# Where a unit's key rows are fetched in a streamed two-layer cross attention

## The chip, the cores and the metric

The kernel runs on one core of a Trainium2 chip. A core has a matrix engine (TensorE, PE in the profile, with weight loads shown as PEld), VectorE (DVE), ScalarE (ACT), GpSimd (POOL) and SyncE (SP). Each runs its own list of instructions in order; semaphores hold an instruction until what it needs is done. Nearly all DMA copies of this kernel are issued by SyncE, one after the other. An issue takes some 0.4 to 0.6 us of SyncE; the copy itself runs on 16 DMA engines. An issue that waits for a semaphore holds up every later issue of SyncE.

The metric is the device time of one execution in microseconds. Before the change it is 3652.42 us, the median of 3 runs (3637.54 to 3652.66).

## The reference

A Perceiver-like stack of two layers works on 32 batches of 64 query tokens of width 256, and attends in each layer to a context of 1601 tokens per batch. Cut to what matters here:

```
x = x + L0_xattn(layernorm(x), ctx, ctx, ...)   # 16 heads of 16, 1601 keys
x = x + L0_attn(layernorm(x), ...)              # self attention over 64 tokens
x = x + L0_ffn(layernorm(x), ...)               # top-k routed attention
x = x + L1_xattn(layernorm(x), ctx, mask, ...)  # cross attention again, masked
x = x + L1_attn(layernorm(x), ...)              # quantised self attention
x = x + L1_ffn(layernorm(x), ...)               # product-key experts
```

In a cross attention, q, k and v are projections of x and of the context, scores are q.k for each head, a softmax runs over the 1601 keys (in layer 1 the masked ones are left out), and the result is the weighted sum of v. Each batch of the context is gone through once per layer, 64 batch passes in all. Almost the whole time goes into these two cross attentions; the small stages of layer 0 are woven in between.

## The kernel before, in words

`stream` (from line 509) does both cross attentions as one stream. The work is cut in **units**: unit `u` is four heads of one batch pass, `b, q4 = divmod(u, 4)`, so there are `NU` = 256 units, some 12 us each. Keys reach a unit in three hops:

- **Projection.** `projections` (L1069) walks 416 pairs of 128-token context blocks, each with index `i`. `load(i)` (L970, issue at L974) brings `raw` into one of three buffers. `split(i)` (L982) makes `chi` on ScalarE (L986) and `clo` on GpSimd (L987). `keys(i)` runs 24 matmuls into `kp` (L1089) and adds the bias on VectorE (L1095); `values(i)` does the same for v (L1117, L1122).
- **Parting.** `parted(i)` (L1032) cuts a key block into three bf16 parts `ks` (ScalarE L1039 and L1046, GpSimd L1040 and L1041) and stores them to a DRAM scratch `kd` (L1049), a ring of four batches.
- **Fetch.** `fetch(u)` (L1187) gathers a unit's rows from `kd` into `kst`, one of three buffers (`kring[u % 3]`): four copies of 208 KB (L1203), four of 104 KB (L1208), 1248 KB together, and in layer 1 a ninth of 25.1 KB with the mask (L1213).

What `keys`, `split` and `parted` have left to do is kept in lists, and `tick()` (L1005) hands out a little of it: first the raw loads that are due, then, for each pending generator, one stage (a parting's first half, its second half, its store, or a split). `fetch(u)` first calls `tick(b)` for its own batch, which hands out a stage of the others too, and finishes all that batch `b` still owes. `keys_values` (L1300) draws further projection steps until a target that grows by a twelfth of a batch per step is met.

The order of everything is written out by hand in the loop over units (L1417). Each iteration has three steps (`i` = 0, 1, 2), and a step is, in this order: maxima of the next unit's scores (`sp`, L1236, VectorE L1241), weighted sums of the last step's probabilities (`acc`, L1292), this step's score products (`tp`, L1277, with ScalarE's exponential `e`, L1282), then `group_step`, `end_step` (small pieces of the other stages; the twelve `qst` copies of L632 that bring new queries every 16 units come from here), `tick()` and `keys_values`. The third step computes the products `p5` and `p6`, the last that read the unit's `kst` buffer, and ends with a second `group_step`.

At the top of iteration `u`, `fetch(u + 2)` is called:

```
                if u + 2 < NU and u + 2 not in ksts:
                    fetch(u + 2)
```

Its buffer is that of unit `u - 1`, whose last products stand in the third step of the iteration before. The first reader of the fetched rows is `maxima(u + 2)`, at the start of iteration `u + 1`. The copies wait on SyncE for those last products and, for a batch's first unit, for the batch's last store to `kd`.

Of the kernel before, what the change touches and what calls it, by code (L numbers as in the profile page):

```python
# [61 lines left out]
class Kernel:  # L62
# [446 lines left out]
    def stream(self):  # L509
        nc, tc, ins = self.nc, self.tc, self.ins  # L510
        with ExitStack() as ctx:
# [25 lines left out]
            def layer(b):  # L537
                return b // NB
# [5 lines left out]
            def halves(x):  # L544
                return x.rearrange("(r p) h n -> r p h n", r=2)
# [446 lines left out]
            kds, vs, ksts, cuts, loads, due = {}, {}, {}, [], [], []  # L992
# [12 lines left out]
            def tick(b=-1):  # L1005


                if b < 0:
                    due[:], rest = loads[:], due[:]
                    del loads[:]  # L1010
                    for one in rest:
                        one()
                left = 2
                for one in list(cuts):
                    work = one[1] == "work"
                    if one[0] > b and work:
                        if left == 0:
                            continue
                        left -= 1
                    while True:  # L1020
                        one[1] = next(one[2], None)
                        if one[1] is None:
                            cuts.remove(one)
                        if one[1] is None or one[0] > b:
                            break
# [161 lines left out]
            def fetch(u):  # L1187

                b, q4 = divmod(u, 4)
                while keyed.get(b, 0) < NCH:  # L1190
                    made[0] += next(proj)
                tick(b)
                k = kring[u % 3]
                if u == 2:

                    for r in (32, 96):
                        nc.sync.dma_start(k[r : r + 32 : 2], kring[0][r : r + 32 : 2])

                kh = halves(k).rearrange("r p (a j) n -> r a p (j n)", a=2)
                d = kds[b][:, 16 * q4 : 16 * q4 + 16]  # L1200
                for rows, part in ((FIRST, 0), (THIRD, 1)):
                    for r in range(2):
                        nc.sync.dma_start(  # L1203
                            halves(k)[r, rows].rearrange("p h n -> p (h n)"), d[part]
                        )
                for a in range(2):
                    for r in range(2):
                        nc.sync.dma_start(  # L1208
                            kh[r, a, SECOND],
                            d[0 if r == a else 2, :, 2 * a * NKP : 2 * a * NKP + 2 * NKP],  # L1210
                        )
                if layer(b) == 1:
                    nc.sync.dma_start(  # L1213
                        k[MASKR : P : 64, :, :NKE],
                        self.rows[b % NB, :NKE].unsqueeze(0).unsqueeze(0)
                        .to_broadcast([2, 4, NKE]),
                    )
                ksts[u] = k
# [48 lines left out]
            def probabilities(u, i):  # L1267

                q, h0, tok = tokens(u)
                k = ksts[u]  # L1270
                two = min(2, NCH - 2 * i)
                m = min(P, NK - 2 * i * P)
                sp = ps_t.tile([P, 2, 4, NQ], F32, tag="tp", name=f"tp{u}_{i}")
                for c in range(two):
                    k0 = (2 * i + c) * P
                    for h in range(4):
                        nc.tensor.matmul(  # L1277
                            sp[:m, c, h, :], k[:, 2 * (h % 2) + h // 2, k0 : k0 + m], q[:, h0 + h, tok],
                            start=True, stop=True,
                        )  # L1280
                e = pt.tile([P, 2, 4, NQ], F32, tag="e", name=f"e{u}_{i}")
                nc.scalar.activation(e[:m, :two], sp[:m, :two], AF.Exp)  # L1282
                return e

            def weighted(u, i, e):

                b, q4 = divmod(u, 4)
                slot = 2 * q4 + b % 2
                for c in range(2 * i, min(2 * i + 2, NCH)):
                    m = min(P, NK - c * P)  # L1290
                    for h in range(4):
                        nc.tensor.matmul(  # L1292
                            acc[32 * h : 32 * h + 17, slot, :], vs[b, c][:m, 4 * q4 + h, :],
                            e[:m, c - 2 * i, h, :], start=(c == 0), stop=(c == NCH - 1),
                        )

            NU = 2 * NB * 4
# [14 lines left out]
            def prepare():  # L1312

                for which, n in (("L1_attn_w_qkv", 24), ("L1_attn_w_out", 8)):
                    got = self.sc.tile([P, n], F32, tag=f"wm{n}", name=f"{which}_m")
                    yield from self.weight_max(bg, which, got)
                    yield from self.weight_grid(which, got, bank)
                    yield from self.weight_round(bg, which)
                yield from self.temperature()

            def end_step():

                for queue in (ends, spare):
                    while queue:
                        n, t, steps = queue[0]
                        if next(steps, True) is None:
                            return
                        queue.pop(0)
                        if n == 1:
                            spare.append((2, t, self.twice_normed(small, bg, t)))  # L1330
                        elif n == 0 and t % 2 == 1:
                            g = t // 2
                            groups.append((128 + 16 * g - 2, self0(g)))
                            groups.append((128 + 16 * g - 1, ffn0(g)))
# [57 lines left out]
            def banks_made(n):  # L1392
                for _ in range(n):
                    made[0] += next(proj)
                    tick()
# [16 lines left out]
            for i, _ in enumerate(maxima(0)):  # L1412
                if i < 4:
                    banks_made(1)
            groups.append((15, self.stream_setup(wp, bg, bank)))
            late = []
            for u in range(NU):  # L1417
                b, q4 = divmod(u, 4)
                if u in (2, 3, 4):
                    self.load_x(1 << (u - 1), 1 << (u - 1))  # L1420
                if u == 133:

                    assert not ends
                    nc.sync.dma_start(
                        self.bo,
                        ins[self.WNAMES[1][3] % "v"].unsqueeze(0).to_broadcast([P, D]),
                    )
                    self.bv.append(self.bo)
                if u in (8, 132):
                    spare.append((2, 0, prepare() if u == 8 else self.affine_grids(bg)))  # L1430
                if u % 16 == 1 and u + 15 < NU:
                    groups.append((u + 15, queries(*divmod((u + 15) // 16, NG))))
                if u + 2 < NU and u + 2 not in ksts:
                    fetch(u + 2)
                nat = maxima(u + 1) if u + 1 < NU else iter(())

                for i, js in enumerate(((0, 1, 2), (3, 4), (5, 6))):
                    for _ in range((2, 2, 0)[i]):
                        next(nat, None)
                    for done in late:  # L1440
                        weighted(*done)
                        if done[1] == 6 and done[0] % 8 == 7:
                            n, t = divmod(done[0] // 8, NT)
                            ends.append((n, t, finish(n, t)))
                            next(ends[-1][2])
                    if i == 2:
                        next(nat, None)
                    late = [(u, j, probabilities(u, j)) for j in js[:2]]
                    banks[0] = 0
                    group_step()  # L1450
                    end_step()
                    tick()
                    keys_values(LEAD + (3 * u + i + 1) / 12.0, 0.15)
                    late += [(u, j, probabilities(u, j)) for j in js[2:]]
                    if i == 2:
                        group_step()
                        if u % 2:
                            end_step()
                for _ in nat:
                    pass  # L1460
# [976 lines left out]
```

## Time and profile before

| what | before |
|---|---|
| median of 3 runs | 3652.42 us (3637.54 to 3652.66) |
| the profiled execution's own time | 3643.7 us |
| its span | 3642.0 us |
| mean granted TensorE clock | 0.956 |
| TensorE busy | 3316.4 us (91%) |
| VectorE busy | 2417.2 us (66%) |
| ScalarE busy | 2367.8 us (65%) |
| GpSimd busy | 1792.4 us (49%) |
| DMA moved | 651.22 MB, 179 GB/s mean |
| `kst` copies from `kd` | 1024 of 208 KB, 1024 of 104 KB |
| `raw` loads | 379 of 256 KB, 62 of 72 KB |
| stores to `kd` | 384 of 384 KB, 64 of 108 KB |

How to read it: the profile is one execution. Its chain of work that ended last runs only through the closing stages here (VectorE 7%, TensorE 2% of the span), so the stream, the first 3090 us or so, is read by the waits of its engines and by their timelines. A line of waits says which engine and line waited, for whom, then the total in us, how many times, and the longest. In a timeline a number in square brackets is the idle time of the engine before an instruction, and what ended it. SPq is SyncE's queue, where an issue's duration is not the copy's. A stretch's line gives busy time of each engine, the granted TensorE clock, the DMA engines' share and GB/s.

### The profile page before, as it was taken

The numbers are of one execution on the slowest core, as the hardware profiler recorded it, in microseconds if no ns is written. First come the engines' busy times: TensorE is split into PE (matmuls) and PEld (weight loads), VectorE is DVE, ScalarE is ACT, GpSimd is POOL, SyncE is SP. The second block draws the span as 40 slices with busy tenths as digits, with TensorE's granted clock in tenths as the row PEclk, the third lists the DMA queues.
The fourth block names the chain that finished last, engine by engine and source line by source line (L and its number), as shares of the span: only waits on it lengthen the run. The fifth ranks groups of instructions, "written<-read, shape, count | busy, mean of one in ns | idle before, by whom it ended". The sixth has DMA issues, their size and how long they took to land. (4 is left out here: it accounts for less than half of the span.)

```text
span 3642.0 us, 148306 instructions
## 1 busy us (share of the span) xinstructions
PE 3316.4 (91%) x62993; PEld 2707.7 (74%) x63007; DVE 2417.2 (66%) x6166; ACT 2367.8 (65%) x4656; POOL 1792.4 (49%) x2109
## 2 busy tenths in 40 slices
PE   6899999999999999999999999999999998775698
PEld 5678887878778787778887778878778786332467
DVE  4556665666666566566667666656666566789879
ACT  3677766767667776667676777677667676154562
POOL 2455454555545554545555655556456563003246
PEclk8999999999999999999999999999999999887699
DMA  7888777777777777777787777777778887100000
GB/s 179 214 231 230 203 191 213 205 207 201 204 193 205 211 208 214 200 198 200 204 216 210 199 209 197 195 210 202 206 206 232 231 241 194 60 1 1 1 5 20
DMA packets 616920, 651.22 MB, mean 179 GB/s; under 512 B 127216, under 2 KB 581444, under 8 KB 599684
## 3 DMA queue, kind: packets, MB, share of 16 engines
q1 hardware_dynamic: 616256, 641.73, 64.3%
q8 instruction: 495, 8.11, 1.0%
q14 instruction: 169, 1.38, 0.1%
HBM read 468.30 MB, written 171.11 MB: 176 GB/s over the span
## 5 line engine op out<-in xcount | busy, mean ns | idle before, releaser
L1241 DVE TENSOR_REDUCE mx<-sp 128x1 f32<-128x400 f32 (+1 forms) x2048 | 1031.8, 565 | 324.5 <-PE sp L1236 323.9
L1282 ACT ACTIVATE e<-tp 128x512 f32<-128x512 f32 (+1 forms) x1792 | 931.7, 565 | 465.4 <-PE tp L1277 456.4
L987 POOL TENSOR_TENSOR clo<-raw,chi 128x512 fp32r<-128x512 f32 (+1 forms) x408 | 508.3, 1246 | 558.7 <-ACT chi L986 552.4
L1040 POOL TENSOR_TENSOR kr<-kr,ks 128x512 f32<-128x512 f32 (+1 forms) x406 | 459.4, 1132 | 608.7 <-ACT ks L1039 570.9
L1095 DVE TENSOR_SCALAR kr<-kp,bk 128x256 f32<-128x256 f32 (+1 forms) x832 | 356.3, 470 | 542.1 <-PE kp L1089 441.0
L1277 PE MATMUL tp<-qst,kst 128*128 128x64 bf16 (+1 forms) x13312 | 579.9, 195 | 15.0 <-ACT e L1282 13.1
L1292 PEld LDWEIGHTS acc<-e,v 128*17 128x17 f32 x26624 | 395.6, 98 | 213.2 <-issue 139.7
L1292 PE MATMUL acc<-e,v 128*17 128x64 f32 x26624 | 540.9, 222 | 13.2 <-ACT e L1282 10.5
L1277 PEld LDWEIGHTS <-kst 128*128 128x128 bf16 (+1 forms) x13312 | 462.2, 100 | 114.8 <-issue 22.0
L1117 PE MATMUL vp<-w_hi,chi 128*128 128x256 f32 (+1 forms) x1664 | 508.0, 305 | 15.7 <-DVE w_hi L222 12.4
L1117 PE MATMUL vp<-w_lo,chi 128*128 128x256 f32 (+1 forms) x1664 | 473.3, 284 | 0.4 <-DVE w_lo L223 0.3
L1117 PE MATMUL vp<-w_hi,clo 128*128 128x256 f32 (+1 forms) x1664 | 473.6, 285 | 0.0
L1041 POOL TENSOR_TENSOR ks<-kr 128x512 bf16<-128x512 f32 (+1 forms) x406 | 413.5, 1018 | 31.9
L1236 PE MATMUL sp<-kst,qst 64*64 64x400 bf16 (+1 forms) x4096 | 319.2, 349 | 92.0 <-DMA kst<-kd 41.2
L1089 PE MATMUL kp<-chi,w_hi 128*128 128x256 f32 (+1 forms) x1664 | 371.3, 305 | 14.4 <-DVE w_hi L222 6.2
L1122 ACT COPY v<-vp 128x512 f32<-128x512 f32 (+1 forms) x416 | 244.8, 588 | 184.9 <-PE vp L1117 181.7
L1089 PE MATMUL kp<-clo,w_hi 128*128 128x256 f32 (+1 forms) x1664 | 339.0, 285 | 15.3 <-POOL clo L987 14.5
L1117 PEld LDWEIGHTS vp<-w_hi,chi 128*128 128x128 f32 (+1 forms) x1664 | 313.9, 189 | 33.5 <-issue 9.5
L1089 PE MATMUL kp<-chi,w_lo 128*128 128x256 f32 (+1 forms) x1664 | 337.4, 285 | 0.0
L986 ACT CAST chi<-raw 128x512 fp32r<-128x512 f32 (+1 forms) x410 | 249.8, 609 | 105.6 <-DMA raw<-in_ctx_dram 105.4
L1117 PEld LDWEIGHTS vp<-w_lo,chi 128*128 128x128 f32 (+1 forms) x1664 | 314.6, 189 | 1.7 <-DVE w_lo L223 0.9
L1117 PEld LDWEIGHTS vp<-w_hi,clo 128*128 128x128 f32 (+1 forms) x1664 | 313.7, 189 | 0.0
(721 smaller groups left out, 5113.0 us busy)
## 6 DMA issues: line engine op xcount, KB each, us to landing
kst<-kd SPq DMA_DIRECT2D x1024, 208.0 KB
kd<-ks SPq DMA_DIRECT2D x384, 384.0 KB
kst<-kd SPq DMA_DIRECT2D x1024, 104.0 KB
raw<-in_ctx_dram SPq DMA_DIRECT2D x379, 256.0 KB
qst<-xa_qd SPq DMA_DIRECT2D x192, 64.0 KB
kd<-ks SPq DMA_DIRECT2D x64, 108.0 KB
xa_qd<-xa_qs SPq DMA_DIRECT2D x16, 384.0 KB
raw<-in_ctx_dram SPq DMA_DIRECT2D x62, 72.0 KB
```

Source lines behind the costliest of these rows:

```text
L986: nc.scalar.copy(hi[:, :, :n], raw[:, :, :n])
L987: (nc.vector if i < 2 else nc.gpsimd).tensor_tensor(lo[:, :, :n], raw[:, :, :n], hi[:, :, :n].bitcast(F32), ALU.subtract)
L1040: eng.tensor_tensor(x, x, ks[:, 0, :, :m], ALU.subtract)
L1041: eng.tensor_tensor(ks[:, 2, :, :m], x, upper(x), ALU.subtract)
L1089: nc.tensor.matmul(kp[:, oc, :m], wk[w][:, cc, oc * P : (oc + 1) * P], x[:, cc, :m], start=(j == 0), stop=(j == 5),)
L1095: nc.vector.tensor_scalar(r[:, oc, :m], kp[:, oc, :m], self.bk[n][:, oc : oc + 1], None, ALU.add,)
L1117: nc.tensor.matmul(vp[:w_, i1, :], x[:, cc, o], wv[w][:, cc, :], start=(j == 0), stop=(j == 5),)
L1236: nc.tensor.matmul(sp[a][64 * j : 64 * j + 64, :n], q[r, h0 + 2 * j + a, tok], k[r, 2 * a + j, k0 : k0 + n], start=True, stop=True,)
L1241: nc.vector.tensor_reduce(mx[:, a, g : g + 1], sp[a][:, :n], AX.X, ALU.max)
L1277: nc.tensor.matmul(sp[:m, c, h, :], k[:, 2 * (h % 2) + h // 2, k0 : k0 + m], q[:, h0 + h, tok], start=True, stop=True,)
L1282: nc.scalar.activation(e[:m, :two], sp[:m, :two], AF.Exp)
L1292: nc.tensor.matmul(acc[32 * h : 32 * h + 17, slot, :], vs[b, c][:m, 4 * q4 + h, :], e[:m, c - 2 * i, h, :], start=(c == 0), stop=(c == NCH ...
```

## The change

The call of `fetch` at the top of an iteration goes. Instead `fetch(u + 3)` is called in the third step of iteration `u`, behind `end_step()` and ahead of `tick()`: after the products `p5` and `p6` of unit `u`, whose buffer it fills, and before the raw loads and key stores that this `tick()` issues, before `keys_values` and before the second `group_step`. `fetch(2)` stands ahead of the loop. So the same fetches are made in the same order, each a part of one step earlier in the program, and `tick(b)` inside `fetch` moves with it.

```diff
             groups.append((15, self.stream_setup(wp, bg, bank)))
+            fetch(2)
             late = []
             for u in range(NU):
...
-                if u + 2 < NU and u + 2 not in ksts:
-                    fetch(u + 2)
                 nat = maxima(u + 1) if u + 1 < NU else iter(())
...
                     group_step()
                     end_step()
+                    if i == 2 and u + 3 < NU:
+
+                        fetch(u + 3)
                     tick()
                     keys_values(LEAD + (3 * u + i + 1) / 12.0, 0.15)
```

## The prediction

> **What bounds the kernel now.** I read the page first, then the waits of TensorE, then the clock by stretches, then the SyncE queue's own timeline beside those of TensorE and ScalarE. The page has TensorE busy 3316.4 of 3642.0 us. By stretches (0:3090 is the streamed stage that the change touches) it is busy 2911.96 of 3090 us, so about 178 us of idle time there is all that an edit to loads can give back directly. The waits of TensorE from 200 to 3090 us, and then from 0 to 200 us, name the loads of unit rows (`kst`) as the largest single cause:
>
> ```profile
> PE sp L1236 <- DMA kst<-rows: 27.5, 14, 4.4
> PE sp L1236 <- DMA kst<-kd: 16.9, 17, 3.3
> PE kp L1089 <- POOL clo L987: 12.1, 16, 2.2
> PE tp L1277 <- ACT e L1282: 11.5, 14, 1.7
> PE sp L1236 <- DMA qst<-xa_qd: 7.2, 3, 2.9
> ...
> PE sp L1236 <- DMA kst<-kd: 24.2, 8, 8.3
> ```
>
> The columns are total us, times, longest. 44.4 us after 200 us, 24.2 before: 68.6 us in which TensorE stands because rows have not landed. The reader should see next why they are late. This is SyncE's timeline ahead of one such stall (unit 58), TensorE's row of the stall, and the stretch behind it (columns: start, us; in the last line the clock is the number after POOL):
>
> ```profile
> 758.52 0.62 SPq L974 DMA_DIRECT2D raw<-in_ctx_dram  x1
> 759.25 0.41 SPq L1049 DMA_DIRECT2D kd<-ks  x1
> 759.71 1.54 SPq L632 DMA_DIRECT2D qst<-xa_qd  x2
> 761.35 3.03 SPq L1203 DMA_DIRECT2D kst<-kd  x4
> 764.42 2.48 SPq L1208 DMA_DIRECT2D kst<-kd  x4
> ...
> 768.39 0.36 PE L1236 MATMUL sp<-kst,qst 64*64 64x401 bf16 x2 [3.27 <-DMA kst<-kd]
> ...
> 769.40:772.80 3.40, 3.40 (x51) 2.58 (x52) 1.54 (x3) 1.08 (x2) 1.50 (x2) 0.50 1.20 361
> ```
>
> The buffer was free at 751.4 (end of the last `tp` of three units before); the fetch started at 761.35 because SyncE was issuing 12 `qst` copies, raw loads and key stores one after another. It costs 5.5 us to issue, lands 1.5 us later, and TensorE loses 3.27 us and then runs 3.40 us at half clock. That is the exception. Going through all 253 fetches from unit 3 on, 135 start within 0.2 us of the last product of the buffer's reader, 78 start more than 2 us later, 41 more than 4. The usual case looks like this (SyncE, then TensorE, then ScalarE):
>
> ```profile
> 1036.54 1.60 SPq L974 DMA_DIRECT2D raw<-in_ctx_dram  x1
> 1038.56 0.37 SPq L1049 DMA_DIRECT2D kd<-ks  x1
> 1040.47 2.39 SPq L1203 DMA_DIRECT2D kst<-kd  x4
> 1042.90 3.53 SPq L1208 DMA_DIRECT2D kst<-kd  x4
> ...
> 1039.90 0.54 PE L1277 MATMUL tp<-qst,kst 128*128 128x64 bf16 x12
> ...
> 1050.37 0.64 ACT L986 CAST chi<-raw 128x512 fp32r<-128x512 f32 x1
> ```
>
> The products end at 1040.44, the fetch starts at 1040.47: here nothing is won by putting it first. And the raw load issued at 1036.54 is read at 1050.37; it is what will be pushed back.
>
> **The change, part by part.** The order of the two programs' instructions shows that TensorE's own order is untouched. What moves:
>
> (a) On SyncE the eight row copies (nine in layer 1) pass what the third step's `tick()` and its second `group_step` issue: 112 of 410 raw loads, 148 key stores, and in bursts two `qst` copies. Ahead of unit 58 that is 0.62 + 0.41 + 1.54 us with gaps, 758.52 to 761.35 = 2.83 us. A stall shorter than that goes; a longer one keeps the rest. Layer 1's 14 stalls are 3.4, 0.7, 3.4, 0.4, 3.3, 2.3, 4.4, 1.5, 2.5, 1.3, 0.3, 0.3, 2.2, 1.5. Five of them (1.3, 0.3, 0.3, 2.2, 1.5) have nothing movable in front: they stay, 5.6. Of the others 0.6 + 0.6 + 0.5 + 1.6 = 3.3 remain. Won: 27.5 - 8.9 = 18.6. Of the 16.9 for `kd` the same count leaves 3 us: won 14. The 7.2 put down to `qst` stand at the same first product of a unit; I take half, 3.6. Before 200 us, unit 0's 8.8 us is loaded ahead of the loop and stays; units 3, 4, 6 and 9 (8.0, 1.7, 4.4, 1.2) have 2.1, 1.6, 4.3 and 1.4 us of issues in front that are passed: won 2.1 + 1.6 + 4.3 + 1.2 = 9. Sum of (a): 45 us. Bounds: nothing, and all of 68.6 - 8.8 + 7.2 = 67.
>
> (b) The clock. The granted clock is 0.50 in nine stretches that begin within 5 us of a `kst` stall (612.4, 769.4, 943.5, 1796.8, 2551.1, 2708.2, 2721.8, 2861.8, 2875.4), 3.4 to 6.8 us long, 37.5 in all: at half speed 18.8 us lost. I expect seven of nine to go: 14 us; bounds 0 and 18.8. The Trainium skill ("TensorE: Matmul & The Clock Gate", "What's actually happening") puts the half clock behind at least one idle window of about 3.4 us. By that rule only stalls of 3.4 us count, some three of them, and (b) would be about 6 us. This trace has a half-clock stretch at 943.5 behind two waits of 0.92 and 1.03 us, so I go by the rows.
>
> (c) The loads that are passed. For each of the 112 raw loads I took from the timelines its issue, its reader's start on ScalarE (median 14.9 us later, least 3.1), and the later of its issue and the buffer's last product, plus 5 us for the fetch now in front: the push is 5 to 13.7 us, median 8.7. With 3 us to land (issue 753.19, reader released 756.43) ten come late, by 19 us in all. ScalarE's waits for raw loads are 105.4 us today:
>
> ```profile
> ACT chi L986 <- DMA raw<-in_ctx_dram: 105.4, 39, 10.3
> SPq L1203 <- PE tp L1277: 195.9, 118, 7.1
> ```
>
> What of such a wait reaches TensorE: from 200 us on its waits for `clo` and `e` are 12.1 + 11.5 + 6.9 = 30.5 against 74.6 of ScalarE's for raw, 0.41 at most, 0.25 without `clo`. So 19 us cost 5 to 8. Nearer the fetch, the raw load of the next unit's first step gets a load and a store (1 to 2 us) in front; 64 of these are split as early as before, and 1.5 us more makes 18 of them late by 15 us: 4 to 6 on TensorE. Against that, `fetch` calls `tick(b)` itself. It now runs directly before the ordinary `tick()`, not after it and `keys_values`, so 111 splits and about a third of the key partings are issued one step (some 4 us) later. 78 of these splits read a first-step load, and these had 44.5 of the 105.4 us: worth 11 to 18. I take (c) as 0; bounds -15 and +45 (next part).
>
> (d) Stores. A key store waits behind the fetch 5 us longer. The last store of a batch keeps its place ahead of the fetch that reads it (SyncE's waits there, 111.6 us in 49 times, stay), and the others have a unit or more of cover. If that cover went, SyncE itself would wait. Cost 0. The head of SyncE now waits for the third step's products (195.9 us in 118 waits, more after), with raw loads, stores and `qst` queued behind it: this is priced in (c). Moving `fetch(2)` ahead of the loop changes no order: 0.
>
> Sum: -45 - 14 + 0 = -59, of which I keep 55, since a stall removed at a unit's first product can show up as one of the 0.3 to 0.9 us waits for VectorE beside it. The profiled execution took 3643.7 us, so 3589; that execution lies 8.7 us under the median of 3652.42, and I put the time at 3595.
>
> **The rivals.**
> 1. Slower: raw loads land late. The place is ScalarE's split of the 112 loads behind the fetch, in-order ahead of `e`. If behind 1248 KB of rows a load lands in 8 us, not 3, 84 of the 112 are late by 220 us; at 0.41 that is 90 on TensorE, less 59: +31, 3675. At 6 us it is 50 loads, 91 us, 37 on TensorE: still a gain of 22. It decides where landing passes about 7 us. Against it: rows issued in 5.5 us land 1.5 us after the last issue, and 361 GB/s were moved in the stretch shown, so the queue drains about as fast as it is filled.
> 2. Hidden anyway: in a burst SyncE has the same copies to issue, so lateness passes from the rows to raw and `qst`, and the stall returns through ScalarE (at 1516.8 ScalarE waited 3.69 us for a raw load and TensorE lost 3.02 us). Only the startup's 9 us and a quarter of the rest, some 12, stay: about 3632 to 3640.
> 3. The change does nothing in most units: true of the 135 fetches that already start at the product, and counted; it can't take more than rival 2 does.
>
> **How the numbers follow.** Forecast (3560 to 3628) 0.65; rival 2 with 3 0.19; rival 1 0.16. About 0.5% (18 us) is what a measurement of this kernel can tell from no change; the three runs of before span 0.4%. Of rival 2 I count 0.07 as faster, 0.11 as same, 0.01 as slower, of rival 1 0.02 as same: faster 0.72, same 0.13, slower 0.15. The low end is all of (a) and (b), 3643.7 - 67 - 18.8 = 3558, so 3560; the high end reaches into the mild part of rival 1, 3660.
>
> **What would show it.** Right: `kst` waits of TensorE under 35 us over the span; fewer than five half-clock stretches between 600 and 3000 us that follow a `kst` stall; SyncE's wait for `tp` at L1203 in clearly more than 118 units; raw waits of ScalarE between 60 and 130 us. Wrong: raw waits over 200 us with TensorE's waits for `e` and `clo` grown by as much as `kst` shrank; or `kst` waits of the same size with SyncE still late by `qst`.

## The result, and the profile after

The changed kernel takes 3714.90 us (median of 5 runs, 3705.59 to 3716.09) against 3652.42 us before: ratio 1.0169, 95% interval 1.0157 to 1.0182. It is slower, by about 62 us. The forecast was 3595 us, faster; the range ended at 3660. The profiled execution after has a span of 3709.2 us at a mean clock of 0.951.

The loss comes little by little. Setting the starts of each unit's first score product in the two traces side by side, the changed kernel is 5.1 us ahead at unit 8, 7.1 behind at unit 72, 33 at unit 152 and 62.6 at unit 255: about 0.3 us per unit on average over most of the stream. So there is no single place to look for.

These are TensorE's waits after the change, from 200 to 3090 us and then, behind the dots at the end, from 0 to 200 us (total us, times, longest):

```profile
PE acc L1292 <- ACT e L1282: 24.9, 32, 2.3
PE sp L1236 <- DMA kst<-rows: 22.4, 11, 3.9
PE kp L1089 <- POOL clo L987: 16.3, 20, 2.1
PE sp L1236 <- DVE mx L1241: 13.6, 25, 0.7
PE sp L1236 <- DMA kst<-kd: 11.6, 13, 2.2
PE rp L1256 <- DVE mm L1250: 10.4, 17, 0.9
PE tp L1277 <- ACT e L1282: 6.4, 4, 2.3
...
PE sp L1236 <- DMA kst<-kd: 14.1, 6, 8.5
```

The rows' waits (`kst`) fell from 68.6 to 22.4 + 11.6 + 14.1 = 48.1 us. The changed kernel's stream ends some 60 us later, behind 3090 us; over the whole span they fell from 68.7 to 52.9 us, little more than a third of what was forecast for them. Three other waits appeared or grew: weighted sums that wait for ScalarE's exponential (24.9), products for the maxima (`sp`) that wait until VectorE has read an earlier tile (13.6), and the row of maxima `rp` (10.4). Before the change these three lines had 6.9, 2.5 and 1.8 us. The waits of ScalarE and SyncE over the whole span:

```profile
ACT chi L986 <- DMA raw<-in_ctx_dram: 134.2, 62, 10.1
ACT ks L1039 <- DMA kd<-ks: 22.1, 12, 6.2
SPq L1203 <- PE tp L1277: 339.4, 126, 8.4
```

Raw loads are later (105.4 before). The second line is a ScalarE that waits until a store has read its `ks` buffer (11.9 before). SyncE stands 339.4 us in front of its first row copy for the products (195.9), with everything else queued behind it. The stretch 0 to 3090 us, with the busy time of TensorE first, has 29 us less of it than the 2911.96 shown before:

```profile
0.00:3090.00 3090.00, 2883.00 (x57694) 2408.43 (x57695) 1940.51 (x4596) 2072.90 (x4231) 1614.18 (x1828) 0.98 0.74 204
```

That work has moved behind 3090 us, and waits are not the whole loss: over the span TensorE is busy 3345.6 us instead of 3316.4 with the same 62993 matmuls on record. So 29 of the 67 us between the two profiled executions are longer busy time. More time at half clock explains about 5 of them (below); the rest is left open here.

### Why the rows are still late

This is SyncE's timeline ahead of unit 58 after the change, the unit that the prediction showed, and behind the last dots TensorE at that unit (start, us, idle time and its releaser in brackets):

```profile
748.33 2.49 SPq L1208 DMA_DIRECT2D kst<-kd  x4
750.93 0.52 SPq L1049 DMA_DIRECT2D kd<-ks  x1
751.49 3.33 SPq L632 DMA_DIRECT2D qst<-xa_qd  x4
754.92 1.35 SPq L974 DMA_DIRECT2D raw<-in_ctx_dram  x1
...
759.39 1.21 SPq L632 DMA_DIRECT2D qst<-xa_qd  x2
760.70 3.26 SPq L1203 DMA_DIRECT2D kst<-kd  x4
764.00 2.48 SPq L1208 DMA_DIRECT2D kst<-kd  x4
766.59 0.53 SPq L974 DMA_DIRECT2D raw<-in_ctx_dram  x1
...
767.77 0.36 PE L1236 MATMUL sp<-kst,qst 64*64 64x401 bf16 x2 [2.17 <-DMA kst<-kd]
769.67 0.53 PE L1236 MATMUL sp<-kst,qst 64*64 64x401 bf16 x6 [1.54 <-DMA kst<-kd]
```

The first line is the end of unit 57's fetch. It too went past a store and two query copies, which now stand between it and unit 58's fetch, so SyncE takes as long from the end of the one to the start of the other as before (9.88 us, 9.54 before). Unit 58's fetch starts at 760.70 us instead of 761.35. Its buffer came free at 753.47 us, with the last product of unit 55, instead of 751.36; measured from there the fetch is 7.23 us late instead of 9.99, nearly all of the 2.83 us that it was to gain. Yet TensorE loses 2.17 + 1.54 = 3.71 us where it lost 3.27: it goes on 3.2 us after the last row copy was issued (766.48 to 769.67), 1.5 us before the change. Why the rows took longer to land is not shown.

Over all 253 fetches, the lateness (start of the fetch less the end of the product that frees its buffer) falls from 449.9 to 400.5 us. With the banks in turn (below), and the same order on SyncE as in the changed kernel, it is 383.8 us against 440.6 of its control. The fetches that start more than 4 us late are 41 before and 44 after, with 298.5 and 298.7 us together (305.6 and 254.1 with the banks in turn). So the rotation takes 11 to 13% off the lateness and leaves the rest: in a burst the same issues still have to be made, and most of them stand ahead of a fetch in either order.

### The profile page after: what moved, and what is told of

Same layout as the page of the kernel before. It is cut to its first block, busy times and chain, and to the rows that moved or that the text cites. A ratio compares the mean times of both kernels' runs of the same rounds, so it can differ in the third digit from the quotient of the medians.

```text
span 3709.2 us, 148370 instructions
## 1 busy us (share of the span) xinstructions
PE 3345.6 (90%) x62993; PEld 2721.1 (73%) x63007; DVE 2440.0 (66%) x6166; ACT 2362.0 (64%) x4656; POOL 1794.7 (48%) x2109
## 5 line engine op out<-in xcount | busy, mean ns | idle before, releaser
L1236 PE MATMUL sp<-kst,qst 64*64 64x400 bf16 (+1 forms) x4096 | 330.0, 350 | 92.5 <-DMA kst<-rows 27.0
L986 ACT CAST chi<-raw 128x512 fp32r<-128x512 f32 (+1 forms) x410 | 250.4, 611 | 134.5 <-DMA raw<-in_ctx_dram 134.2
```

Of the source, the lines that this page charges most:

```text
L986: nc.scalar.copy(hi[:, :, :n], raw[:, :, :n])
L1236: nc.tensor.matmul(sp[a][64 * j : 64 * j + 64, :n], q[r, h0 + 2 * j + a, tok], k[r, 2 * a + j, k0 : k0 + n], start=True, stop=True,)
```

## The experiments

Ratios are to the kernel before on the same chip, with 95% intervals. A letter in an expectation names a theory of that run alone.

### The rows early, the hand-out where it was

The change moves two things: SyncE's row copies, and the call `tick(b)` inside `fetch`, which hands out splits and partings to ScalarE, GpSimd and VectorE. Here only the first is kept. `owed(b)` finishes what batch `b` itself still owes and hands out nothing else. Against the changed kernel:

```diff
-                tick(b)
+                (tick if u < 3 else owed)(b)
...
+                if 0 < u < NU - 2:
+                    tick((u + 2) // 4)
                 nat = maxima(u + 1) if u + 1 < NU else iter(())
```

> The row copies stand where the change put them, but the call that hands out pending splits and partings stays at the top of the next iteration, so ScalarE, GpSimd, VectorE and TensorE run the order of before and only SyncE's order is that of the change. Theory P (the pace: two hand-outs side by side and then none make ScalarE late): 0.2 to 0.8% faster than before, ScalarE's wait for raw 100 to 140 us, TensorE's acc wait for e about 10 us as before. Theory R (the rows in front of raw loads and stores make ScalarE late): slower than before by 1 to 2%, acc wait for e 25 us or more.

Measured: 3680.65 us, ratio 1.0099 (1.0074 to 1.0124). The order of instructions on TensorE, VectorE, ScalarE and GpSimd is that of the kernel before; only SyncE's differs. So more than half of the loss is there without a new hand-out. Its waits over the span:

```profile
ACT chi L986 <- DMA raw<-in_ctx_dram: 156.1, 67, 9.8
PE tp L1284 <- ACT e L1289: 43.3, 35, 5.1
ACT ks L1039 <- DMA kd<-ks: 23.7, 19, 5.8
PE sp L1243 <- DMA kst<-rows: 19.2, 14, 2.9
PE sp L1243 <- DMA kst<-kd: 18.9, 14, 8.0
```

The rows' waits have fallen by 30.6 us (68.7 to 38.1), the products' waits for `e` have risen by 30.2 (13.1 to 43.3), and ScalarE waits 51 us longer for raw loads. The time is about theory R's, the place is not: the sums wait 14.8 us for `e` (10.5 before), not 25 or more; the products do.

### The hand-out of the change alone

The kernel before, with its fetch where it was, but the projection steps and `tick(b)` of unit `u + 3` directly ahead of the third step's `tick()`:

```diff
+            def paced(u):
+                b = u // 4
+                while keyed.get(b, 0) < NCH:
+                    made[0] += next(proj)
+                tick(b)
...
                     end_step()
+                    if i == 2 and u + 3 < NU:
+                        paced(u + 3)
                     tick()
```

> The other half alone: the rows are copied at the top of the iteration as before, but the hand-out that belonged to the fetch is made in the third step directly ahead of the ordinary one, so ScalarE's and GpSimd's order is that of the change. Theory P: slower than before by 1.5 to 2.5% (it has the loss and not the gain of the earlier rows), TensorE's acc wait for e 25 us or more. Theory R: within 0.5% of before, acc wait for e about 10 us.

Measured: 3697.07 us, ratio 1.0147 (1.0130 to 1.0164). The prediction had credited the hand-out with a gain. But one wait is much longer here than in either of the two kernels it stands between. SyncE, and TensorE behind the dots:

```profile
SPq L1049 <- ACT ks L1046: 425.4, 113, 9.4
...
PE sp L1242 <- DMA kst<-kd: 53.1, 35, 8.5
```

A key store now stands at the head of SyncE right behind the parting that fills it (256.8 us before, 23.6 in the changed kernel), and the rows are queued behind it. So its 1.5% is not the price of the hand-out in the changed kernel. Neither theory had this: the time is near P's, but the sums wait 15.5 us for `e`, not 25 or more.

### Raw loads first, stores first, or both first

Three kernels from the first one, with the rows behind the raw loads that are due, behind the stores, or behind both. `brought()` is the part of `tick()` that issues the due raw loads, and `tick(bring=False)` is the rest of it:

```diff
-                    if i == 2 and u + 3 < NU:
-                        fetch(u + 3)
-                    tick()
+                    early = i == 2 and u + 3 < NU
+                    if early:
+                        brought()
+                        fetch(u + 3)
+                    tick(bring=not early)
```

> As e1, but in the third step the raw loads that are due are issued ahead of the rows; stores stay behind them. Theory P: as e1 or up to 0.3% faster, ScalarE's raw wait near or below the 105 us of before. Theory R with raw loads as the cause: within 0.5% of before; with the stores as the cause: as slow as e1.

Measured: 3659.53 us, ratio 1.0039 (1.0024 to 1.0054).

```diff
-                    if i == 2 and u + 3 < NU:
-                        fetch(u + 3)
-                    tick()
+                    early = i == 2 and u + 3 < NU
+                    if early:
+                        tick(bring=False)
+                        fetch(u + 3)
+                        brought()
+                    else:
+                        tick()
```

> The mirror of e3: stores ahead of the rows, due raw loads behind them. Theory that each kind costs what the other left: slower by 0.4 to 0.8%, ScalarE's waits for raw 140 us or more, its ks waits for kd stores back near the 5 us of before (units 30 to 250). Theory that stores are the larger part: within 0.3% of before.

Measured: 3659.75 us, ratio 1.0052 (1.0033 to 1.0070).

```diff
-                    if i == 2 and u + 3 < NU:
-                        fetch(u + 3)
                     tick()
+                    if i == 2 and u + 3 < NU:
+                        fetch(u + 3)
```

> Rows stand behind the third step's raw loads and key stores, ahead of keys_values and of the second group step, so they pass only qst copies and small loads; the hand-out stays as before. If passing raw loads (about 0.6% by e1 less e3) and passing stores (about 0.4%, what e3 left) are all of e1's loss: within 0.5% of before, or faster by up to 0.5%, TensorE's kst waits 50 us or less and ScalarE's waits for raw near 105 us. If earlier rows harm by themselves (DMA traffic): still 0.4% slower or more.

Measured: 3636.47 us, ratio 0.9983 (0.9970 to 0.9996). With the rows a part of a step earlier than before, but behind the loads and stores of that place (they still pass 6 of the 148 stores, and no raw load), the loss is gone and a small gain is left. What `tick()` issues must not be passed. This kernel's waits:

```profile
ACT chi L986 <- DMA raw<-in_ctx_dram: 107.9, 36, 10.3
PE tp L1284 <- ACT e L1289: 33.1, 25, 3.8
PE sp L1243 <- DMA kst<-kd: 30.4, 20, 8.2
PE sp L1243 <- DMA kst<-rows: 10.6, 7, 2.8
```

The rows wait 27.7 us less than before (68.7 to 41.0) although nearly nothing is passed but query copies and small loads, and ScalarE's waits for raw loads are as before (105.4). But the products wait 20.0 us longer for `e` (13.1 to 33.1) and the sums 3.6 (10.5 to 14.1). So most of what the rows win is met by longer waits for ScalarE, and 6 us of time are left; why `e` is later there, with the raw loads as before, is not shown.

How the loss splits between loads and stores can't be read from the times of the two runs between, because a third thing differs in them too, which showed only later (below). Their waits do tell which passing makes which wait:

| kernel | ScalarE for raw loads | ScalarE for `ks` buffers held by stores |
|---|---|---|
| rows first | 156.1 | 23.7 |
| raw loads, then rows, then stores | 115.1 | 27.8 |
| stores, then rows, then raw loads | 169.7 | 8.6 |
| loads and stores, then rows | 107.9 | 9.0 |

### Take the query copies off SyncE

The bursts come from twelve `qst` copies in every sixteenth unit. In the kernel before, and in the one with the rows behind the loads and stores, GpSimd issues them:

```diff
-                        nc.sync.dma_start(
+                        nc.gpsimd.dma_start(
                             parity(qh[r, rows], a),
```

> The kernel before, with the twelve qst copies of each 16 units issued by GpSimd and not SyncE. If the row stalls come from SyncE's backlog of qst copies, as the prediction read them, TensorE's kst waits after 200 us fall from 44 to under 20 us and the kernel is faster by 0.5 to 1.2%. If the rows are late for another reason: kst waits stay, same time or slower by what GpSimd's issues cost.

> e4 with the qst copies on GpSimd. If SyncE's backlog is the cause of the late rows, there is little left to pass, and this equals e6 within 0.3%; if the place of the rows matters by itself, it is faster than e6 by 0.3% or more.

Measured: 3580.36 us, ratio 0.9824 (0.9804 to 0.9844), and 3574.28 us, ratio 0.9811 (0.9788 to 0.9834). The kernel before with this edit alone:

```profile
ACT chi L986 <- DMA raw<-in_ctx_dram: 33.9, 20, 4.5
PE sp L1236 <- DMA kst<-kd: 17.5, 10, 7.1
PE tp L1277 <- ACT e L1282: 6.5, 12, 1.1
PE sp L1236 <- DMA kst<-rows: 6.3, 4, 3.5
```

Rows wait 23.8 us instead of 68.7, raw loads 33.9 instead of 105.4, and little has grown in their place (`kp` for `clo`, 14.5 to 21.7). The second kernel is within 0.3% of the first, as expected if little is left to pass. The diagnosis of the prediction (rows are late because of these bursts) was right; the remedy was not. The Trainium skill ("Trainium Kernel Development and Optimization", "Key Constraints") says that DMAs from several engines' queues share the same 16 DMA engines, so that issuing from several saves only the issue time. Here issue time is what was short: the 192 issues take 0.60 us of SyncE each in the median, some 115 us, in bursts, and saving it was worth 1.8% (whether the other queue that the copies now run in helps too was not tried apart).

### Is the loss made in the bursts?

The same edit in the changed kernel and in the one with the rows early:

> The changed kernel with the twelve query copies of every sixteenth unit issued by GpSimd instead of SyncE. Theory A (what is lost comes from the bursts: with SyncE crowded by the query copies, the rows, raw loads and stores only exchange places): the bursts are gone, so are their victims, and the time is within 0.4% of the kernel before with the same one-line edit, 0.9824: 0.980 to 0.986. Theory B (the loss is in every unit: raw loads and stores behind 1248 KB of rows, and the hand-out bunched at one place): it stays beside the gain, 0.9824 + 0.017, so 0.996 to 1.002. ScalarE's waits for raw loads: by A under 50 us, by B over 80; TensorE's first product for p4's exponential (34 us in the changed kernel): by B still over 25.

> The kernel with the rows early and the hand-out where it was, again with the query copies on GpSimd. By theory A 0.980 to 0.986, as the one beside it. By theory B the loss from passing raw loads and stores stays, 0.9824 + 0.010: 0.990 to 0.995. A mixed result, this one at 0.982 and the one beside it at 0.988 or above, says that passing costs only in bursts, and that the bunched hand-out costs in every unit.

Measured: 3639.24 us, ratio 0.9980 (0.9966 to 0.9993), and 3621.78 us, ratio 0.9933 (0.9912 to 0.9954). The times are theory B's: the loss stands beside the gain. The waits are not: ScalarE waits 49.0 and 62.7 us for raw loads, not over 80, and the sums wait 15.0 us for `e` in the changed kernel, not over 25. Something else is lost outside the bursts, and one of the lines that stayed names it, here from the changed kernel with this edit:

```profile
PE sp L1236 <- DVE mx L1241: 15.0, 27, 0.7
```

Before the change it is 2.5 us in 4 times. Such a wait is 0.50 us long in the median where it stops a unit's fourth tile (19 of the 27), and falls inside a unit's first score products. TensorE at unit 185 of the changed kernel, and behind the dots VectorE:

```profile
2369.16 0.53 PE L1236 MATMUL sp<-kst,qst 64*64 64x401 bf16 x6
2370.18 0.36 PE L1236 MATMUL sp<-kst,qst 64*64 64x400 bf16 x2 [0.50 <-DVE mx L1241]
...
2369.55 2.02 DVE L1241 TENSOR_REDUCE mx<-sp 128x1 f32<-128x401 f32 x4 [0.48 <-PE sp L1236]
```

The unit's first four tiles take the PSUM banks 5, 6, 2 and again 5 in the compiled program, so the fourth waits until VectorE has read the first. Before the change the same four have 4, 3, 5 and 6. The order of instructions on TensorE and VectorE is the same in both. The kernel asks a pool of five buffers for each tile (`bank`, L550 to L552), and which bank a tile gets is settled when the program is built. Of the pool's 3592 tiles that take a used bank:

| kernel | bank of five tiles earlier | of four or fewer earlier | ratio measured |
|---|---|---|---|
| before | 3483 | 62 | 1 |
| the change | 3043 | 366 | 1.0169 |
| rows early, hand-out as before | 3099 | 310 | 1.0099 |
| hand-out of the change alone | 3438 | 99 | 1.0147 |
| raw loads first | 3188 | 268 | 1.0039 |
| stores first | 3253 | 201 | 1.0052 |
| rows behind loads and stores | 3470 | 72 | 0.9983 |

### The banks in turn

To have the same banks in all kernels, each tile gets its own tag of one buffer, five tags in turn:

```diff
+            turn = [0]
...
-                return ps_m.tile([P, 512], F32, tag="mm", name=name)
+                turn[0] += 1
+                return ps_m.tile([P, 512], F32, tag=f"mm{turn[0] % 5}", name=name, bufs=1)
```

Then every tile has the bank of five tiles earlier, and all these kernels have the same banks. The control is the kernel before:

> The control: the kernel before with the banks in turn. 3483 of its 3592 tiles already have the bank of five tiles earlier, so both theories expect little: 0.995 to 1.004.

Measured: 3642.39 us, ratio 1.0006 (0.9993 to 1.0019).

> The kernel with the rows early and the hand-out where it was, with the banks in turn. Theory A: its 1.0099 goes to 0.985 to 1.000. Theory B: 1.006 to 1.012. Mixed: whatever this one keeps above the control beside it is the cost of passing raw loads and stores, and what the changed kernel keeps above this one is the cost of the hand-out at one place.

Measured: 3661.65 us, ratio 1.0055 (1.0036 to 1.0074).

> The changed kernel with the five PSUM banks of the score and projection tiles taken strictly in turn, instead of as the build assigns them. In the compiled programs the build gave a tile a bank that had been written four or fewer tiles earlier 62 times of 3592 before the change and 366 times after it (310 with the rows early and the hand-out in its old place, 72 with the rows behind the loads and stores). Theory A (the loss is this: tiles of TensorE wait for a bank whose last reader has only just begun): 0.990 to 1.002 of the kernel before, TensorE's waits for the maxima in front of score products under 6 us, against 15.0. Theory B (the loss is what the change does to the loads, the stores and the hand-out): it stays at 1.012 to 1.020.

Measured: 3683.04 us, ratio 1.0103 (1.0080 to 1.0126). Neither theory: about four tenths of the loss are the banks, the rest is not. The score tiles' waits for VectorE's maxima (15.0 us in the changed kernel) are gone altogether; what else the banks cost is not put down to a line here. The place shown above, in the changed kernel with the banks in turn (6, 2, 3 and 4), has no wait:

```profile
2347.05 0.54 PE L1238 MATMUL sp<-kst,qst 64*64 64x401 bf16 x8
2347.51 0.53 PE L1294 MATMUL acc<-e,v 128*17 128x64 f32 x24
```

What is left can now be compared line by line with the control, since only the queues and the hand-out differ. The control first, then the rows early with the old hand-out, then the changed kernel, all with the banks in turn:

```profile
ACT chi L988 <- DMA raw<-in_ctx_dram: 97.5, 37, 9.7
PE sp L1238 <- DMA kst<-kd: 40.9, 26, 7.5
PE sp L1238 <- DMA kst<-rows: 27.4, 15, 3.9
PE tp L1279 <- ACT e L1284: 17.2, 20, 2.1
ACT ks L1041 <- DMA kd<-ks: 10.6, 7, 6.1
```

```profile
ACT chi L988 <- DMA raw<-in_ctx_dram: 163.0, 66, 9.6
PE tp L1286 <- ACT e L1291: 43.8, 33, 4.7
ACT ks L1041 <- DMA kd<-ks: 26.3, 19, 4.9
PE sp L1245 <- DMA kst<-kd: 22.0, 14, 8.1
PE sp L1245 <- DMA kst<-rows: 14.7, 12, 4.3
```

```profile
ACT chi L988 <- DMA raw<-in_ctx_dram: 130.6, 58, 9.1
PE acc L1294 <- ACT e L1284: 21.7, 43, 2.3
PE sp L1238 <- DMA kst<-kd: 21.9, 18, 7.2
PE tp L1279 <- ACT e L1284: 17.0, 15, 3.4
PE sp L1238 <- DMA kst<-rows: 16.1, 11, 3.7
PE rp L1258 <- DVE mm L1252: 12.4, 19, 1.0
```

From the first to the second, the rows' waits fall by 31.6 us (68.3 to 36.7), ScalarE waits 65.5 us longer for raw loads and 15.7 for stores that hold its `ks` buffers, and TensorE's waits for `e` rise by 26.6 at the products alone. From the second to the third, raw loads wait 32.4 us less and the products 26.8 less, but `rp` now waits 12.4 us for VectorE at this line (the second has no such wait), the sums 5.3 us more (16.4 to 21.7), and the kernel is still slower. Of the second kernel's 43.8 us at the products, the kernel with the rows behind the loads and stores has 33.1 already, with raw waits of 107.9; so passing adds some 11 us there and 55 us of raw waits.

The fastest kernel with the banks in turn:

> The fastest so far (rows behind the loads and stores of that place, query copies on GpSimd, 0.9811) with the banks in turn. Its banks are nearly in turn already (3468 of 3592), so both theories expect 0.977 to 0.985.

Measured: 3569.97 us, ratio 0.9800 (0.9786 to 0.9815), the fastest of this study and faster than both kernels.

### Passing and hand-out without bursts

> The kernel with the rows early and the hand-out in its old place, banks in turn, query copies on GpSimd. Theory C: 0.9800 + 0.0055, so 0.983 to 0.988. Theory D: 0.978 to 0.982. If this one is at 0.980 and the one beside it at 0.986, passing costs only in bursts and the hand-out in every unit.

> The changed kernel with the banks in turn and the query copies on GpSimd: neither of the two other causes is left. Beside it stands the same with the rows behind the loads and stores, 0.9800. Theory C (passing loads and stores, and the bunched hand-out, cost in every unit): 0.9800 + 0.0103, so 0.988 to 0.993. Theory D (they cost only where the query copies crowd SyncE): 0.979 to 0.985.

Measured: 3589.34 us, ratio 0.9844 (0.9818 to 0.9871), and 3609.77 us, ratio 0.9902 (0.9883 to 0.9921). These are theory C's times: both costs are there without the bursts too.

So the loss comes apart into four steps, each a ratio of two runs (intervals from theirs, added as squares); beside it the same steps where GpSimd issues the query copies:

| step | with the bursts | without |
|---|---|---|
| rows earlier, passing no load and 6 of 148 stores | 0.9983 +- 0.0013 | 0.9987 +- 0.0030 |
| they also pass the raw loads and stores | 1.0055 / 0.9983 = 1.0072 +- 0.0023 | 0.9844 / 0.9800 = 1.0045 +- 0.0031 |
| the hand-out moves with them | 1.0103 / 1.0055 = 1.0048 +- 0.0030 | 0.9902 / 0.9844 = 1.0059 +- 0.0033 |
| the build assigns other banks | 1.0169 / 1.0103 = 1.0065 +- 0.0026 | 0.9980 / 0.9902 = 1.0079 +- 0.0024 |

In the column with the bursts that is -6, +26, +17 and +24 us of 3643, 61 together. The product is 1.0169 by construction; that the right column repeats it is the test. The first step of the right column is 0.9811 / 0.9824. The runs of the first row, and 0.9983 in the second, have the build's banks, with 62 to 73 tiles in a bank of four or fewer tiles earlier; the control (1.0006) and the pair 0.9811 and 0.9800 put that at some 0.1%.

## Why the prediction was wrong, step by step

**(a) The rows, -45 us: half of it in the waits, 6 us in the time.** In the changed kernel the `kst` waits fell from 68.7 to 52.9 us over the span and the one put down to `qst` (7.2) is gone: 23 us. With the banks held the same it was 30.3 (68.3 to 38.0). Two steps failed. One is the counting of stalls one by one, with all else left where it was: unit 58's fetch did pass its 2.8 us, but its buffer came free later, its rows landed later, and TensorE stood longer. The other is the allowance for waits that return, 4 us of 59 and only for VectorE: in the kernel that passes no raw load the rows' waits fell by 27.7 us, the waits for ScalarE's `e` rose by 23.6, and the time fell by 6.

**(b) The clock, -14 us: none.** Between 600 and 3000 us eight of 19 half-clock stretches still have a wait for `kst` at their start or in the 6 us before (ten of 18 before the change), and all of them together are 78.5 us instead of 68.3. The place of one stall is taken by others: in the changed kernel a stretch begins at 1217.8 us behind waits of 0.74 and 0.41 us. The idle window of about 3.4 us that the Trainium skill names ("TensorE: Matmul & The Clock Gate", "What's actually happening") would not have foretold that one. The term itself failed with (a): it took the stalls of the rows to go away.

**(c) The loads that are passed, 0: the step that decides the sign.** It was a difference of two terms. The push was expected to cost 19 + 15 us of ScalarE's waits and some 9 to 14 of TensorE's. ScalarE's waits for raw loads rose by 55 us against the kernel that passes none (65.5 against the control), and loads and stores passed together cost 26 us; some 11 of them are seen at the products, the others are not put down to a line. The mechanism was right, and so was the landing: where ScalarE waits over 0.5 us for a raw load issued within 1.5 us behind a fetch, its split starts 3.45 us after the issue (median of 30; 3.26 before the change, median of 15). But of the 410 splits of a raw buffer 96 now start less than 5 us after its last load was issued, 61 before, and where the split is late, ScalarE's exponentials behind it are too. The hand-out was credited with 11 to 18 us. It did shorten the raw waits (by 32.4 us), and it costs 17: VectorE's `mm` and ScalarE's `e` for the sums come later. Which piece of the hand-out delays which is read from the waits, and was not tried apart.

**(d) The stores, 0: mis-sized.** The cover named there (a unit or more for all but a batch's last store) was counted for the reader of the store. The writer was left out: ScalarE's next parting needs the `ks` buffer, and its waits for that rose from 10.6 to 26.3 us. The waits of SyncE for a batch's last store, which were to stay at 111.6 us in 49 times, are 178.9 in 70 in the changed kernel: the fetch comes to the head of the queue earlier and waits there, with the raw loads behind it. What of the 26 us is the stores' was not measured apart, and a kernel with more `ks` buffers was not tried.

**Not in the sum: the banks, +24 us.** The prediction argued that TensorE's own order is untouched, which is true, and had no term for what TensorE writes to. The compiled program's waits show the difference before any run: 28 times a unit's fourth score tile waits there for VectorE instead of ScalarE.

**The rivals.** Rival 1 had the sign and the place, raw loads late in front of `e`, but not the mechanism (landing did not slow to 7 us), and its price had to be set against a gain that was too large. Rival 2 named what happened to the rows' gain: most of it was lost again in waits for ScalarE, and the kernel that passes no raw load gained about 6 us. It ended near no change since it priced neither the passing outside the bursts nor the banks. (Its time takes off 12 us only; the startup's 9 and the 12 together would have given 3623 to 3631.) Rival 3 doesn't hold: the passing and the hand-out cost something without the bursts too (1.0045 and 1.0059). The signs named at the end spoke clearly: `kst` waits of 52.9 us, not under 35, and raw waits of 134.2, just over 130, with more waiting for `e`.

## What to carry to other kernels

When a queue is full in bursts, moving one unit's copies ahead of other work on it takes little off their own lateness (11 to 13% here) and hands more to that work; what is won at one wait can be lost at another (24 of 28 us here). Better take issues off the queue instead (here 1.8%, from one line). A buffer's price has two ends: for every transfer that is pushed back, ask who reads its result and who needs its source buffer. And compare the compiled programs' waits and buffer assignments, not only the order of instructions: an edit that touches none of an engine's work can still give it other buffers.

## What the runs showed of the hardware that was not expected

- A tile written into a PSUM bank whose reader has just begun costs TensorE 0.50 us here in the median where it is a unit's fourth (0.66 to 0.72 where it is the second or third). The Trainium skill ("Perfetto Trace Analysis", "Matmuls") asks to rotate independent products through different banks; the runs put 0.4 to 1.0% on doing so in 3592 of 3592 cases instead of some 3050.
- GpSimd issues a `qst` copy of 64 KB in about 0.5 us of its own busy time (1889.4 - 1792.4 = 97.0 us for 192 copies). Of TensorE's waits, the one for GpSimd's `clo` grew beside it from 14.5 to 21.7 us.
- Behind a fetch of 1248 KB a raw load lands hardly later than elsewhere: 3.45 us from issue to its reader, against 3.30 where no fetch stands just in front (medians of 30 and 20 waits over 0.5 us in the changed kernel).
